# Cross-attention on one core: the order of the value passes, the engine of a subtraction, a second buffer, and where the bias is loaded

## The chip, the core and the metric

The kernel runs on one core of a Trainium2 chip. The metric is the device time of one execution in microseconds; the figure given for a kernel is the median of its runs. A profiled execution gives the trace from which the durations below are taken. Engines are named as in the profile: PE (TensorE matmuls), PEld (its weight loads), DVE (VectorE), ACT (ScalarE), POOL (GpSimd), SP (SyncE, which only issues transfers here).

## The reference

There are 32 batches of 512 queries with 640 channels, and 77 context tokens of 1024 channels for each batch. The inputs are float32.

```python
q = heads(x @ to_q_w)                    # 20 heads of 32 channels
k = heads(ctx[:, :77] @ to_k_w)
v = heads(ctx[:, :77] @ to_v_w)
h = softmax(q @ k.T / sqrt(32)) @ v      # the object, other and ip parts have no tokens here
out = merge(h) @ to_out_w + to_out_b + x
```

The context has exactly 77 tokens, so the three other attentions of the reference run over no keys and add nothing.

## The kernel before

**Numbers.** Matmul operands are held as two parts in a reduced float32 format: a high part (a rounding copy) and a low part (the source less the high part). A product is three matmuls: high by high, high by low, low by high (`PAIRS`). The helper `split` (L104 to L106) makes the parts: ACT copies the high part (L105), DVE subtracts for the low part (L106). Some places make the low part on POOL instead.

**The order is the program's own.** Every engine works its instructions in the order in which the code records them; nothing is rearranged. An instruction that waits holds up all that stands behind it on its engine. SP issues nearly all transfers, also in order.

**First stage: the context.** The 2464 context rows (32 x 77) go through in five groups `g` of 512 (the last has 416). `load_context` brings a group into `cs`, `context` transposes it (L169) and splits it into eight chunks `ct`, `keys` multiplies it with the key weights (L193, `pk`), `values_of` with the value weights (L193, `pv`), each for five chunks `j` of 128 channels, that is of four heads. `split_keys` splits a chunk of keys into `ks` and stores it to `k_dram` (L214). `split_values` transposes a chunk of values from PSUM into `vt` (L228), splits `vt` into slots 0 and 2 of `vs` (L231; slot 1 stays zero), and stores `vs` to `v_dram` with four transfers (L234). There is one `vt` and one `vs`. In a group, `split_values` of the chunks 0 to 3 stands ahead of the splits of the next group's context chunks 1 to 7, on ACT and on DVE. While a group is split, the query weights (`split_wq`) or the output weights (`split_wo`, stored to `wo_dram`, L323) are split between. The bias, one row of 640 spread over 128 partitions, is loaded at L310 in this stage, between the last weights and the second group's context.

**Second stage: 160 slots.** Slot `n` is batch `b` and chunk `j` of four heads. In it PE makes the scores of the slot, four tiles of 128 queries (`scores`, L452), and the queries of the next one (`queries`, L433). DVE takes the maximum of each tile (L460), ACT the exponentials (`exps`, L470). The slot also works on earlier slots:

- slot n-1: DVE inverts the sums (`sums`, L480), POOL multiplies (`normalize`, L485), DVE transposes the result into `z` (L492), SP stores it to `pd`, and `load_p` brings it back as `raw` with keys on the partitions (L508, L509);
- slot n-3 (`taken`): `cast_p` rounds the probabilities of the rows 0 to 255 of `raw` on ACT (L516: parts 0 and 1 of `pp`); `rest_p` rounds the 64 remaining rows on ACT (L522) and subtracts for parts 2 and 3 on DVE (L523); `last_p` subtracts for the 64 rows on POOL (L530). Part 4 of `pp` so holds the rest rows, high and low. `values` multiplies with the values `vb` (L544): for each half `p` of PSUM tile `pa` three passes, with the parts `p`, `2 + p` and 4. `sum_a` brings `pa` together into `aw` (ACT L555, DVE L557 twice), and `split_a` splits `aw` into `at`: ACT copies (L566), POOL subtracts (L567);
- the batch before: `piece` multiplies `at` with the output weights (L584, `po`), `finish` adds the residual and stores (L613), `add_bias` adds the bias to the residual on POOL (L577).

In some of the five slots of a batch the next batch's `x` is transposed on DVE (`transpose_x`, L256) and split, high on ACT and low on POOL (`split_x`, L263, L264). The order on the engines at the seam of two slots is: `sum_a`, exps of the last tile, `split_a`; then the next slot's `cast_p`, its first scores with L460, `rest_p`, `sums`, `normalize` and `last_p` (in the first slots, `last_p` ahead of `normalize`). The five value chunks of the last context group are made just before and in the first two slots (`context_values`). `end` finishes the last three takes.

Of the kernel before, what the change touches and what calls it, by code (L numbers as in the profile page):

```python
# [8 lines left out]
F32 = mybir.dt.float32  # L9
FPR = mybir.dt.float32r  # L10
AF = mybir.ActivationFunctionType
ALU = mybir.AluOpType
# [11 lines left out]
P = 128  # L24
Q = 32
HEADS = 20
HD = 32
# [24 lines left out]
def kernel(  # L52
# [25 lines left out]
    nc = tc.nc  # L78
    B, S, C = x.shape
# [6 lines left out]
    G = 512  # L86
# [5 lines left out]
    const = ctx.enter_context(tc.tile_pool(name="const", bufs=1))  # L92
# [5 lines left out]

    v_dram = dram.tile([NT + KPAD - NKEY, HPC, NC_, 3, HD], FPR, name="v_dram")
    wo_dram = dram.tile([P, NC_, 2, C], FPR, name="wo_dram")  # L100

    bias = const.tile([P, C], F32, name="bias")

    def split(hi, lo, src):  # L104
        nc.scalar.copy(hi, src)  # L105
        nc.vector.tensor_tensor(lo, src, hi.bitcast(F32), ALU.subtract)  # L106

    def load_weights(w, k0, kn, permuted=True, queues=(nc.sync,) * 4, tag="wraw"):


        raw = kvw.tile([P, 2, C], F32, tag=tag, name="wraw", bufs=3 if tag == "wraw" else 2)
        if permuted:
            rows = w.rearrange("(q c i) n -> q i c n", q=4, i=Q)
            for q, queue in enumerate(queues):
                queue.dma_start(raw[q * Q : (q + 1) * Q, :kn], rows[q, :, k0 : k0 + kn])
        else:
            rows = w.rearrange("(c p) n -> p c n", p=P)
            nc.sync.dma_start(raw[:, :kn], rows[:, k0 : k0 + kn])
        for k in range(kn):
            wraws[id(w), k0 + k] = raw[:, k]  # L120
# [15 lines left out]
    kvp = tc.alloc_tile_pool(name="kvp", bufs=1, side="right")  # L136
# [12 lines left out]
    cts, pks, pvs, css, craws, wraws = ({} for _ in range(6))  # L149
# [73 lines left out]
    def split_values(g, j, between=None):  # L223

        g0, gn = GROUPS_KV[g]
        na = gn // Q
        vt = kvp.tile([P, G], F32, tag="vt", name="vt", bufs=1)
        nc.vector.transpose(vt[:, :gn], pvs.pop(j)[:, :gn])  # L228
        if between is not None:
            between()  # L230
        split(vs[:, :na, 0], vs[:, :na, 2], vt[:, :gn].rearrange("p (a d) -> p a d", d=HD))  # L231
        dst = v_dram[g0 : g0 + gn, :, j].rearrange("(a t) i c d -> i t a (c d)", t=Q)
        for i in range(HPC):
            nc.sync.dma_start(  # L234
                dst[i].bitcast(F32),
                vs[i * Q : (i + 1) * Q, :na].rearrange("p a c d -> p a (c d)").bitcast(F32),
            )

    def context_values(g, j, pool):
        values_of(g, j, pool)  # L240
        split_values(g, j)
# [25 lines left out]
    ctx.enter_context(tc.manual_schedule(engines=ENGINES))  # L267


    vs = kvp.tile([P, G // Q, 3, HD], FPR, name="vs")  # L270
    nc.gpsimd.memset(vs.bitcast(F32), 0.0)
    zero = kvt.tile([P, 2, G], FPR, name="zero", tag="ks")[:, 0]
    nc.vector.memset(zero.bitcast(F32), 0.0)
    warm = psk.tile([P, G], F32, tag="ps", name="warm")
# [30 lines left out]
    for k in range(2, NK, 2):  # L305
        first(k, k + 1)
        if k < 6:
            load_weights(wk, k + 2, 2)
            load_weights(wv, k + 2, 2)
    nc.sync.dma_start(bias, bo.unsqueeze(0).to_broadcast([P, C]))  # L310
    LAST, split_ks = len(GROUPS_KV) - 1, []

    def split_wq():
# [16 lines left out]
    for g in range(LAST):  # L330
        for j in range(NC_):
            if g or j > 2:
                values_of(g, j, psk)
            if not g and j < 3:
                split_keys(0, j)
            if not g and j == 2:
                continue
            if j == 1:
                context(g + 1, 0)
            if not g and j == 3:  # L340
                split_values(0, 2)
                split_keys(0, 3)
            if j == NC_ - 1:
                if not g:
                    context(g + 1, 1, 2)
                    split_keys(0, 4)
                context(g + 1, *range(1 if g else 3, NK))
                if g + 1 == LAST:
                    kvw.release()
                    kvc.release()  # L350
                    xpool.append(
                        ctx.enter_context(
                            tc.tile_pool(name="xpool", bufs=1, reuse_waits="tile")
                        )
                    )
                    load_x(0)
            split_values(g, j, (None, split_wq, split_wo, None)[g])
# [28 lines left out]
    main = ctx.enter_context(tc.tile_pool(name="main", bufs=1, reuse_waits="tile"))  # L386
# [3 lines left out]

    raws, pps, ats, pds, sms, pqs, pas, aws, xrs, pos = ({} for _ in range(10))

    kbs, vbs, pnb = [], [], []
    for g, (j0, nj) in enumerate(GROUPS):
        kb = main.tile([P, nj, 2, KCOLS], FPR, name=f"kb{g}")
# [137 lines left out]

    PASSES = [(p, t, c) for p in range(2) for t, c in ((0, p), (0, 2 + p), (1, 4))]

    def values(n):
        b, j = divmod(n, NC_)
        g = GROUP_OF[j]  # L540
        pp, vb = pps.pop(n), vbs[g][:, j - GROUPS[g][0]]
        pas[n] = late[1].tile([P, 2, S], F32, tag="pa", name="pa", bufs=1)
        for m, (p, t, c) in enumerate(PASSES):
            nc.tensor.matmul(  # L544
                pas[n][:, p, :],
                vb[:, p, t, :],
                pp[:, c, :],
                start=(m % 3 == 0),
                stop=(m % 3 == 2),
            )  # L550

    def sum_a(n):
# [7 lines left out]
    def split_a(n):  # L560
        if n >= N - NC_ + 1:
            at = xpool[0].tile([P, 2, S], FPR, tag="xt", name="at", bufs=7)
        else:
            at = late[0].tile([P, 2, S], FPR, tag="at", name="at", bufs=8)
        aw = aws.pop(n)
        nc.scalar.copy(at[:, 0, :], aw[:, 0])  # L566
        nc.gpsimd.tensor_tensor(at[:, 1, :], aw[:, 0], at[:, 0, :].bitcast(F32), ALU.subtract)  # L567
        ats[n] = at

    def load_residual(b, t, xr=None):  # L570
# [66 lines left out]
    def take(m):  # L637
        values(m)
        sum_a(m)
        split_a(m)  # L640
# [14 lines left out]
    def slot(n, beside=()):  # L655
# [76 lines left out]
        if taken is not None:  # L732
            values(taken)
# [14 lines left out]
        if taken is not None:  # L748
            split_a(taken)
# [145 lines left out]
```

## Time and profile before

| | |
|---|---|
| median of 3 runs | 2183.4 us (2183.16 to 2183.89) |
| the profiled execution | 2184.32 us, its span in the profile 2182.5 us |
| PE | 1959.6 us busy (90%), mean granted clock 0.982 |
| ACT | 1545.2 us (71%) |
| DVE | 1414.8 us (65%) |
| POOL | 1207.1 us (55%) |
| first stage, up to the first slot's scores | about 314 us |
| L567, POOL's subtraction | 160 of 1293 ns, 206.9 us |
| L544, value matmuls | 960 |

A line of the waits reads: engine, tile and line of the one that waited, `<-` the one that ended the wait; total us, times, longest. A line of the timeline reads: start and duration in us, engine, line, operation, output from inputs with their shapes, and in brackets the idle time before it and who ended it. Matmuls overlap, so PE's busy time is not time at its peak; the pitch from start to start says more.

### The profile page before, as it was taken

The page shows a single profiled execution, that of the slowest core. Times are in us where ns is not written, and L with a number is a line of the kernel's source. Part 1 is how long each engine was busy: PE and PEld are TensorE (multiplying, and loading weights), DVE is VectorE, ACT ScalarE, POOL GpSimd, SP SyncE. Part 2 cuts the span into 40 slices and gives each one's busy share as a digit, 9 for nine tenths or more (in the row PEclk, how much of TensorE's full clock was granted, in tenths as well). Part 3 has the DMA queues.
Part 4 walks back from the last instruction along what each step waited for, and adds up shares of the span by engine and source line. Part 5 has one row for each costly group of instructions (what it writes and reads, how often), then busy time and mean ns, then how long its engine had stood idle before and what let it go on. Part 6 is the DMA issues. An engine that isn't in the chain of part 4 may idle for free. (4 is left out here: it accounts for less than half of the span.)

```text
span 2182.5 us, 36539 instructions
## 1 busy us (share of the span) xinstructions
PE 1959.6 (90%) x10332; PEld 1697.8 (78%) x10332; DVE 1414.8 (65%) x2174; ACT 1545.2 (71%) x6210; POOL 1207.1 (55%) x807
## 2 busy tenths in 40 slices
PE   9787987899999999999999999999999999999997
PEld 7566886777777777887778777787777877778786
DVE  4342344777777777777777777777777777777763
ACT  3131136887887877878788888888788887888872
POOL 1000024666666666666666666666666666666654
PEclk9899999999999999999999999999999999999998
DMA  9658677887878888888888788888888887877874
GB/s 190 147 149 212 153 158 206 218 204 205 204 202 206 203 208 206 209 204 204 208 205 208 197 211 209 205 201 206 208 207 207 205 201 204 203 203 206 202 187 133
DMA packets 568280, 431.28 MB, mean 198 GB/s; under 512 B 195344, under 2 KB 477072, under 8 KB 568080
## 3 DMA queue, kind: packets, MB, share of 16 engines
q1 hardware_dynamic: 564848, 417.65, 76.8%
q0 software_dynamic: 3136, 11.14, 1.4%
q8 instruction: 84, 1.38, 0.3%
q14 instruction: 116, 0.95, 0.1%
q10 hardware_dynamic: 96, 0.16, 0.0%
HBM read 247.17 MB, written 181.64 MB: 196 GB/s over the span
## 5 line engine op out<-in xcount | busy, mean ns | idle before, releaser
L470 ACT ACTIVATE pn<-sc,nm 128x77 f32<-128x77 f32 x2560 | 801.6, 333 | 74.1 <-DVE nm L460 70.2
L584 PE MATMUL po<-wo_s,at 128*128 128x320 f32 x3840 | 627.4, 312 | 10.2 <-DVE xr L613 3.6
L433 PE MATMUL pq<-xt,wq_s 128*128 128x512 f32 x2400 | 607.7, 394 | 0.6 <-POOL xt L264 0.6
L584 PEld LDWEIGHTS po<-wo_s,at 128*128 128x128 f32 x3840 | 579.4, 190 | 20.2 <-DVE xr L613 15.0
L470 ACT ACTIVATION_READ_ACCUMULATOR pn<-sc,nm 128x1 f32 x2560 | 541.3, 211 | 0.0
L433 PEld LDWEIGHTS pq<-xt,wq_s 128*128 128x128 f32 x2400 | 437.5, 189 | 76.9 <-POOL xt L264 1.7
L485 POOL TENSOR_TENSOR pn<-pn,rs 128x1232 f32<-128x1232 f32 x160 | 364.0, 2275 | 231.7 <-DVE rs L480 231.3
L567 POOL TENSOR_TENSOR at<-aw,at 128x512 fp32r<-128x512 f32 x160 | 206.9, 1293 | 417.4 <-ACT at L566 255.2
L460 DVE TENSOR_REDUCE nm<-sc 128x4 f32<-128x308 f32 x640 | 291.9, 457 | 215.1 <-PE sc L452 204.9
L544 PE MATMUL pa<-pp,vb 128*128 128x512 f32 x960 | 293.6, 415 | 149.7 <-POOL pp L530 146.2
L452 PE MATMUL sc<-kb,qt 128*128 128x308 f32 x1920 | 379.4, 306 | 14.9 <-ACT pn L470 13.3
L452 PEld LDWEIGHTS sc<-kb,qt 128*128 128x128 f32 x1920 | 325.1, 189 | 61.1 <-ACT pn L470 14.7
L523 DVE TENSOR_TENSOR pp<-raw,pp 128x1024 fp32r<-128x1024 f32 x160 | 252.5, 1578 | 173.8 <-ACT pp L516 173.8
L544 PEld LDWEIGHTS pa<-pp,vb 128*128 128x128 f32 x960 | 162.6, 189 | 233.6 <-POOL pp L530 215.1
L555 ACT COPY aw<-pa 64x1024 f32<-64x1024 f32 x160 | 161.9, 1012 | 223.0 <-PE pa L544 214.3
L492 DVE STREAM_TRANSPOSE z<-pn 128x1280 f32<-128x1280 f32 x160 | 241.8, 1511 | 120.1 <-POOL pn L485 89.2
L557 DVE TENSOR_TENSOR aw<-pa,aw 64x512 f32<-64x512 f32 x320 | 216.0, 675 | 30.0 <-ACT aw L555 27.7
L264 POOL TENSOR_TENSOR xt<-xs,xt 128x512 fp32r<-128x512 f32 x160 | 204.0, 1292 | 49.3 <-ACT xt L263 47.6
L530 POOL TENSOR_TENSOR pp<-raw,pp 64x512 fp32r<-64x512 f32 x160 | 208.1, 1301 | 20.6 <-ACT pp L522 8.6
L577 POOL TENSOR_TENSOR xr<-xr,bias 128x640 f32<-128x640 f32 x128 | 200.7, 1569 | 9.7
L193 PE MATMUL pk<-ct,wk_s 128*128 128x512 f32 (+1 forms) x600 | 146.2, 403 | 42.1 <-ACT ct L105 34.3
L193 PEld LDWEIGHTS pk<-ct,wk_s 128*128 128x128 f32 x600 | 119.2, 200 | 67.4 <-ACT ct L105 36.2
(42 smaller groups left out, 1415.7 us busy)
## 6 DMA issues: line engine op xcount, KB each, us to landing
pd<-z SPq DMA_DIRECT2D x640, 160.0 KB, 3.1
raw<-pd SPq DMA_DIRECT2D x160, 512.0 KB, 3.9
xs<-in_x_dram SPq DMA_DIRECT2D x128, 320.0 KB, 5.6
xr<-in_x_dram SPq DMA_DIRECT2D x128, 320.0 KB, 3.3
out_dram<-xr SPq DMA_DIRECT2D x127, 320.0 KB, 3.3
raw<-pd SPq DMA_DIRECT2D x160, 128.0 KB, 4.2
v_dram<-vs SPq DMA_DIRECT2D x80, 192.0 KB, 3.9
k_dram<-ks POOLq DMA_DIRECT2D x20, 512.0 KB, 3.4
```

What stands on the lines that cost most here:

```text
L193: nc.tensor.matmul(held[j][:, :gn], w[:, k, a, :], cts[g, k][:, c, :gn], start=(k == 0 and n == 0), stop=(k == NK - 1 and n == 2),)
L433: nc.tensor.matmul(pqs[n], wq_s[:, k, a, j * P : (j + 1) * P], xts[b, k][:, c, :], start=(k == 0 and m == 0), stop=(k == NC_ - 1 and m == 2),)
L452: nc.tensor.matmul(sc[:, :KCOLS], qt[:, a, t * P : (t + 1) * P], kb[:, j - GROUPS[g][0], c], start=(m == 0), stop=(m == 2),)
L460: nc.vector.tensor_reduce(nm, sc[:, :KCOLS].rearrange("p (h k) -> p h k", k=NKEY), AX.X, ALU.max, negate=True)
L470: nc.scalar.activation(pnb[n % 2][:, at, :NKEY], sc[:, i * NKEY : (i + 1) * NKEY], AF.Exp, bias=nm[:, i : i + 1], accum_out=sms[n][:, at : ...
L485: nc.gpsimd.tensor_tensor(pf, pf, rs.unsqueeze(2).to_broadcast([P, NQ * HPC, NKEY]), ALU.mult)
L492: nc.vector.transpose(z.rearrange("p b t j -> p t b j"), pn.rearrange("p (t h) k -> p t (h k)", t=NQ).rearrange("p t (b i) -> p t b i", i=Q),)
L523: nc.vector.tensor_tensor(pp[:, 2:4, :], raw[:, 0:2, :], pp[:, 0:2, :].bitcast(F32), ALU.subtract)
L530: nc.gpsimd.tensor_tensor(pp[64:, 4, :], raw[:64, 2, :], pp[:64, 4, :].bitcast(F32), ALU.subtract)
L544: nc.tensor.matmul(pas[n][:, p, :], vb[:, p, t, :], pp[:, c, :], start=(m % 3 == 0), stop=(m % 3 == 2),)
L557: nc.vector.tensor_tensor(aw[64 * p : 64 * p + 64, 0], pa[:64, p], aw[:64, p], ALU.add)
L584: nc.tensor.matmul(pos[b, t, h][:, :HALF], ats[b * NC_ + j][:, a, t * P : (t + 1) * P], wos[0][:, j, c, h * HALF : (h + 1) * HALF], start= ...
```

## The change

- `PASSES`: the six value matmuls of a slot are reordered. The two that read part 4 of `pp` come last; both PSUM halves are open at the same time.
- `split_a` uses `split`: the low part of `at` is now subtracted on DVE in place of POOL.
- Two buffers `vs`, used in turn by the chunk's number; the transpose writes straight into slot 2 of `vs`, and the low part is subtracted in place; `vt` is gone. Both buffers are cleared on POOL at the start.
- `bias` moves from the constant pool to the second stage's pool, and its load from the first stage to just ahead of the first `load_keys`. The tiles of the second stage lie 2.5 KB further in each partition; in the built program, POOL's clearing of the first key buffer now waits for PE, where before only that of the second did.

```diff
-    bias = const.tile([P, C], F32, name="bias")
...
     def split_values(g, j, between=None):
         g0, gn = GROUPS_KV[g]
         na = gn // Q
-        vt = kvp.tile([P, G], F32, tag="vt", name="vt", bufs=1)
-        nc.vector.transpose(vt[:, :gn], pvs.pop(j)[:, :gn])
+        vs = vss[j % 2]
+        vt = vs[:, :na, 2].bitcast(F32)
+        nc.vector.transpose(vt, pvs.pop(j)[:, :gn].rearrange("p (a d) -> p a d", d=HD))
         if between is not None:
             between()
-        split(vs[:, :na, 0], vs[:, :na, 2], vt[:, :gn].rearrange("p (a d) -> p a d", d=HD))
+        split(vs[:, :na, 0], vs[:, :na, 2], vt)
...
-    vs = kvp.tile([P, G // Q, 3, HD], FPR, name="vs")
-    nc.gpsimd.memset(vs.bitcast(F32), 0.0)
+    vss = [kvp.tile([P, G // Q, 3, HD], FPR, name=f"vs{n}") for n in range(2)]
+    for vs in vss:
+        nc.gpsimd.memset(vs.bitcast(F32), 0.0)
...
-    nc.sync.dma_start(bias, bo.unsqueeze(0).to_broadcast([P, C]))
...
+    bias = main.tile([P, C], F32, name="bias")
+    nc.sync.dma_start(bias, bo.unsqueeze(0).to_broadcast([P, C]))
     kbs, vbs, pnb = [], [], []
...
-    PASSES = [(p, t, c) for p in range(2) for t, c in ((0, p), (0, 2 + p), (1, 4))]
+    PASSES = [(p, 0, p + c) for p in range(2) for c in (0, 2)] + [(p, 1, 4) for p in range(2)]
...
                 vb[:, p, t, :],
                 pp[:, c, :],
-                start=(m % 3 == 0),
-                stop=(m % 3 == 2),
+                start=(c == p),
+                stop=(t == 1),
...
         aw = aws.pop(n)
-        nc.scalar.copy(at[:, 0, :], aw[:, 0])
-        nc.gpsimd.tensor_tensor(at[:, 1, :], aw[:, 0], at[:, 0, :].bitcast(F32), ALU.subtract)
+        split(at[:, 0, :], at[:, 1, :], aw[:, 0])
         ats[n] = at
```

## The prediction

> **What bounds the kernel now.** I read the waits first, then the timeline of one steady slot, then the timeline of the part before the slots. Of the waits:
>
> ```profile
> POOL at L567 <- ACT at L566: 255.2, 100, 4.9
> POOL pn L485 <- DVE rs L480: 231.3, 155, 18.2
> PEld pa L544 <- POOL pp L530: 215.1, 155, 3.7
> ACT aw L555 <- PE pa L544: 214.3, 154, 7.2
> DVE pp L523 <- ACT pp L516: 173.8, 159, 3.0
> PE pa L544 <- POOL pp L530: 146.2, 150, 3.3
> ACT vs L105 <- DMA v_dram<-vs: 84.5, 14, 9.3
> ```
>
> Columns are total us, times, longest. Every engine waits in every slot for the next one: PE for POOL's L530, ACT for PE's L544, DVE for ACT's L516, POOL for DVE's L480. No engine is full; one closed loop through all four sets the period. The timeline of a slot shows it:
>
> ```profile
> 488.13 0.48 DVE L460 TENSOR_REDUCE nm<-sc 128x4 f32<-128x308 f32 x1
> 488.19 0.62 ACT L566 CAST at<-aw 128x512 fp32r<-128x512 f32 x1 [0.24 <-DVE aw L557]
> 488.71 1.04 ACT L516 CAST pp<-raw 128x1024 fp32r<-128x1024 f32 x1
> 488.88 1.29 POOL L567 TENSOR_TENSOR at<-aw,at 128x512 fp32r<-128x512 f32 x1 [3.03 <-ACT at L566]
> 489.79 1.47 DVE L523 TENSOR_TENSOR pp<-raw,pp 128x1024 fp32r<-128x1024 f32 x1 [1.18 <-ACT pp L516]
> 491.50 2.28 POOL L485 TENSOR_TENSOR pn<-pn,rs 128x1232 f32<-128x1232 f32 x1 [1.32 <-DVE rs L480]
> 493.85 1.28 POOL L530 TENSOR_TENSOR pp<-raw,pp 64x512 fp32r<-64x512 f32 x1
> 493.98 0.63 PE L544 MATMUL pa<-pp,vb 128*128 128x512 f32 x2
> 495.18 1.20 PE L544 MATMUL pa<-pp,vb 128*128 128x512 f32 x4 [0.57 <-POOL pp L530]
> ```
>
> The loop: L566, L516, L523, L480, L485, L530, four value matmuls, then L555, L557 and L566 again. The six value matmuls are cut 2 + 4: the third is the first that reads the rest rows, and it starts 0.05 us after L530 ends. L567 starts with L516 and is not in the loop, but it overlaps L523. That costs:
>
> ```profile
> 357.64 1.22 DVE L523 TENSOR_TENSOR pp<-raw,pp 128x1024 fp32r<-128x1024 f32 x1 [3.02 <-ACT pp L516]
> ...
> 477.96 1.29 POOL L567 TENSOR_TENSOR at<-aw,at 128x512 fp32r<-128x512 f32 x1
> ...
> 478.32 2.01 DVE L523 TENSOR_TENSOR pp<-raw,pp 128x1024 fp32r<-128x1024 f32 x1 [0.47 <-ACT pp L516]
> ```
>
> L523 takes 1.22 us with POOL idle at its start, 1.47 where L567 runs 0.38 us into it, 2.01 where it runs 0.93 into it. In both overlapped rows L523 ends 1.08 us after L567, so VectorE does nothing while GpSimd holds on.
>
> The steady slots repeat every five (56.95 us), from the L530 that ends at 403.72 to the one at 2132.57: 1728.85 us, 30.4 periods. PE's wait between the second and third value matmul, less their normal 0.235 us pitch, is 0.55, 0.73, 1.13, 1.49, 1.75 us in the five slots.
>
> Before the slots, PE stands still at each group of the context:
>
> ```profile
> 207.90 0.62 ACT L105 CAST vs<-vt 128x512 fp32r<-128x512 f32 x1 [6.85 <-DMA v_dram<-vs]
> 209.27 2.79 SPq L234 DMA_DIRECT2D v_dram<-vs  x4
> 215.99 0.62 ACT L105 CAST vs<-vt 128x512 fp32r<-128x512 f32 x1 [6.85 <-DMA v_dram<-vs]
> 218.71 0.79 PE L193 MATMUL pk<-ct,wk_s 128*128 128x512 f32 x1 [12.79 <-ACT ct L105]
> ```
>
> The one vs is refilled only when its store has landed, some 7 us a chunk (8.1 here, where a wo store shares the queue); the next context chunk's cast stands behind that on ACT, and PE behind the cast. PE's stalls of this kind: 5.78 + 8.26, 8.89, 12.79 and 4.37, in sum 40.1 us.
>
> **The value passes.** Four matmuls now stand before the wait, two after. Now the third to sixth start 0.05, 0.39, 0.63 and 0.86 us after L530 and the last ends at 1.255; two would end at 0.39 + 0.40 = 0.79. The loop gains 0.465 us. The two moved ahead take 0.47, which fits the smallest stall, 0.55. PE's work per slot is unchanged.
>
> **VectorE's low part.** POOL loses 160 x 1.29 us that nobody waits for. DVE gains 160 x 0.65 (the same subtraction from SBUF, ct at L106: 653 ns), in order behind L557 and ahead of the next slot's L460 (0.48) and L523. It must wait for L566. Queued behind it: that L460, whose maximum is wanted only after L516 and L522, and L523, which is in the loop. From L566's end (488.81): DVE starts at +0.03 (as L523 does after L516), ends at +0.68; L460, overlapping 0.08 as neighbours on DVE do, ends at +1.08; L523 can start at +1.01. Today L516 releases it at +0.98. So ScalarE's cast covers the insertion but for 0.03. Then L523 takes 1.22 instead of 1.47, as POOL is idle: it ends at +2.22 instead of +2.44. Gain 0.22. Bounds: -0.1 (L523 as long as now, and late) to +0.28. I take 0.22, from the 1.22 row. If L516's cover were gone, the whole 0.65 + 0.40 would be on the path.
>
> One slot in five is worse. There POOL's three xt subtractions (474.20, 3.79 us) run until 5.41 us after L530's end, but L566 would end at 4.76 - 0.465 = 4.295. The new subtraction waits 1.115 for POOL, ends 0.515 after that, and L460 and L523 follow: +3.17 instead of today's +2.98. That slot gains 0.465 - 0.19 = 0.27; bounds 0 to 0.5.
>
> Sum: 4 x (0.465 + 0.22) + 0.27 = 3.0 us a period, 30.4 periods: 91 us. Next late would be PE: the 0.73 stall falls to 0.04, the others stay open; ACT's shortest idle time before L555 is 0.59, with 0.3 more in front of its second exps, and DMA's share rises from 0.81 to 0.86. With the ends of the bounds: 1.2 (0.365 x 4, and -0.24) to 3.5 a period, 38 to 106 us.
>
> [...]
>
> **Two vs buffers.** A chunk now waits for the store before the last, and it is VectorE's transpose that waits, not ScalarE's copy. Queued behind it on DVE are the same splits as today. The transpose's strided output I leave at 0.70 (L169 and L492 also stride). Stores issued one after the other land about 1.0 us apart, 4.1 a chunk. Second group: first store issued 125.71, landed 132.3; second landed 136.4; the fourth chunk's copy at 137.2 instead of 146.65, 9.5 earlier, so all of 8.89 goes. First group: 67.8 with a k store between, copy at 68.6 instead of 80.76: 12.2 of the 14.04. Third, with wo stores: 205.8 instead of 215.99: 10 of 12.79. Fourth: 4.4, all. Sum 35.5 us. After each stall the matmuls run at a 427 ns pitch instead of 227 for a while: the 105 that follow take 26.4, 25.9 and 27.0 us, not 23.8, and the fourth group loses 2.0. I count this whole where the stall goes and half where 1.8 and 2.8 us stay: 2.1 + 2.0 + 1.3 + 1.6 = 7. Together 42 us; bounds 14 (stores queue so that a third of the stalls goes) and 50 (all).
>
> [...]
>
> In the first slots the last chunk's copy waits 9.31 us for its store (ACT, 347.05) and PE 5.58 behind it (350.09): 5.6 gained. The second memset, 1.4 us on POOL, delays eight wv loads, whose copies (ACT, 8.26 and 12.90) PE first reads at 13.92 and 19.36: taken as 0, at most 1.4.
>
> **Bias later.** Its load leaves a place where nothing waited and stands on SP between the last k store and the first kb loads, which land at 313.51 to 314.19; PE's scores start at 314.31. No cover: 327 KB at 190 GB/s, 1.7 us. First used at 403.8. So 5.6 - 1.7 = 4 net, bounds -2 to 8. The first kb memset now waits for PE, 1.1 us; kb's loads were issued 5 us later behind other SP work, so 0.
>
> **The end.** The last pieces wait 0.85 us for L567 once, and one value pass moves earlier: 1.5, bounds 0 to 2.5.
>
> **Sum.** 91 + 42 + 4 + 1.5 = 138.5. The profiled execution took 2184.3 us (span 2182.5 and 1.8 around it): 2045.8. The median of the runs is 0.9 less: 2045.
>
> **Rivals.** (1) The loop closes elsewhere for L523: GpSimd's absence does not shorten it, so only the order pays: 63 + 42 + 5.5, 2073. For: nothing but the few 1.22 to 1.45 rows of the first slots shows a free L523. 18%. (2) The stores bound the context stage and the wait only moves to DVE: 14 for 42, 2073. For: DMA share 0.56 to 0.72 there, far from idle. 13%. (3) More is freed, as the PE stalls left (2.6 a period) and the clock allow: about 2015. 6%. (4) Slower: the new subtraction and the L460 behind it lie wholly on the loop, 1.05 + 0.03 less 0.465, 0.615 x 152 = 93 lost against 47.5 gained elsewhere: 2229. It decides for slower once the path grows by 0.465 + 0.31 = 0.78 a slot. Against it: L516's 1.04 us, which runs at that time on another engine. 4%. (5) No change, these cancelling: 1%. The forecast has 58%.
>
> The range reaches over rivals 1 and 2 and the bounds of the terms, short of all bad ends at once (2117): 2018 to 2105. A measurement of this kernel can tell about 0.2%, 4.4 us, from no change. Faster 0.95, same 0.01, slower 0.04.
>
> **What would show it.** Right: 54 us for five slots; pa's matmuls cut 4 + 2, the wait under half its 146 us; L523 near 1.22; L567's successor on DVE just ahead of an L460; no PE stall over 3 us between the groups. Wrong: L523 still 1.47; L523 released by DVE's own queue more than 0.2 us after L516; PE stalls that now name DVE's transpose waiting for v_dram.

## The result, and the profile after

The kernel after takes 2056.65 us (median of 4 runs, 2056.36 to 2058.63), against 2183.49 us before: ratio 0.9421, 95% interval 0.9405 to 0.9437. The forecast was 2045, in a range from 2018 to 2105. The profiled execution's span is 2054.2 us instead of 2182.5: 128.3 us less, where the sum said 138.5.

Cut at the two marks that the prediction used (the L530 of the fifth and of the 157th take; the line is L531 after), the gain stands like this, in us:

| stretch of the span | before | after | gain | forecast |
|---|---|---|---|---|
| to the first scores | 314.32 | 272.37 | 41.95 | 42 |
| first slots, to the first mark | 89.40 | 83.71 | 5.7 | 4 |
| steady slots, between the marks | 1728.85 | 1649.42 | 79.4 | 91 |
| end | 49.93 | 48.7 | 1.2 | 1.5 |
| five steady slots | 56.91 | 54.30 | 2.61 | 3.0 |

So all that is missing lies in the steady slots. The waits of the kernel after (total us, times, longest; most lines left out):

```profile
POOL pn L486 <- DVE rs L481: 442.5, 94, 11.6
...
ACT aw L556 <- PE pa L545: 164.9, 156, 8.3
DVE at L104 <- ACT at L103: 135.3, 160, 1.0
...
PEld pa L545 <- POOL pp L531: 127.8, 153, 3.4
...
PE pa L545 <- POOL pp L531: 55.8, 82, 2.9
...
DVE vs L227 <- DMA v_dram<-vs: 19.2, 7, 4.5
```

PE's wait for the rest rows fell from 146.2 to 55.8 us, as foretold under half. The wait for the store of vs (84.5 us on ACT before) is 19.2 us and now DVE's. The first line is long because POOL has lost work and arrives early; by itself that costs nothing. The timeline of one steady slot (start, duration, engine, line; idle time before it and who ended it in brackets; here and in the later timelines, rows that play no part are left out, also where no dots stand):

```profile
990.88 0.62 ACT L103 CAST at<-aw 128x512 fp32r<-128x512 f32 x1 [0.98 <-DVE aw L558]
991.41 1.05 ACT L517 CAST pp<-raw 128x1024 fp32r<-128x1024 f32 x1
991.53 0.69 DVE L104 TENSOR_TENSOR at<-aw,at 128x512 fp32r<-128x512 f32 x1 [0.74 <-ACT at L103]
992.14 0.47 DVE L461 TENSOR_REDUCE nm<-sc 128x4 f32<-128x308 f32 x1
992.53 1.22 DVE L524 TENSOR_TENSOR pp<-raw,pp 128x1024 fp32r<-128x1024 f32 x1
993.66 0.25 DVE L481 RECIPROCAL rs<-sm 128x16 f32<-128x16 f32 x1
...
994.05 2.27 POOL L486 TENSOR_TENSOR pn<-pn,rs 128x1232 f32<-128x1232 f32 x1 [5.75 <-DVE rs L481]
...
996.26 1.09 PE L545 MATMUL pa<-pp,vb 128*128 128x512 f32 x4
...
996.41 1.28 POOL L531 TENSOR_TENSOR pp<-raw,pp 64x512 fp32r<-64x512 f32 x1
...
997.74 0.73 PE L545 MATMUL pa<-pp,vb 128*128 128x512 f32 x2 [0.39 <-POOL pp L531]
```

The value matmuls are cut 4 + 2 and end 0.785 us after L531 (before 1.255). DVE's new subtraction and L461 fit under ACT's L517 as worked out: L524 starts 1.03 us after the cast into at, takes 1.22 and ends 2.25 after it (forecast 2.22, before 2.45). But look at the reciprocal and normalize: L481 ends at 993.91 (its start and 0.25), L486 starts at 994.05, 0.144 us later. Before, L480 and L485 stood 0.078 us apart:

```profile
1003.46 0.24 DVE L480 RECIPROCAL rs<-sm 128x16 f32<-128x16 f32 x1
...
1003.78 2.27 POOL L485 TENSOR_TENSOR pn<-pn,rs 128x1232 f32<-128x1232 f32 x1 [1.33 <-DVE rs L480]
```

The prediction does not have this step, and it is in the loop in every slot. The built program shows a difference there too. Before, 153 of the 160 normalize instructions wait for DVE alone: L567, ahead of them on POOL, had already waited for an ACT instruction later than the exponentials. After, with no L567, 123 wait for DVE and ACT, 31 for DVE, ACT and an earlier POOL instruction. The starts follow: 0.144 us with two waits, about 0.17 in the slots with three. The trace shows where the time goes. An instruction of its own on POOL's sequencer, which only waits, now stands ahead of every normalize (kernel before, then after; duration in ns as smallest, median and largest, then first and last start in us):

```profile
L485 POOLq EVENT_SEMAPHORE  x7: 17/17/43, 328.3 to 2139.7; - x7
L486 POOLq EVENT_SEMAPHORE  x160: 17/17/43, 285.3 to 2011.9; - x160
```

In the kernel after, it is this instruction that waits for DVE, the wait that ends last, and normalize itself waits for ACT, which has long been done. It ends 0.052 us after the reciprocal, and normalize starts 0.092 us after that. Where it waits for both DVE and ACT it takes 0.043 instead of 0.017 us.

### The profile page after: what moved, and what is told of

It is laid out like the page before. It is cut to its first block, busy times and chain, and to the rows that moved or that the text cites. A ratio compares the mean times of both kernels' runs of the same rounds, so it can differ in the third digit from the quotient of the medians.

```text
span 2054.2 us, 36186 instructions
## 1 busy us (share of the span) xinstructions
PE 1952.5 (95%) x10332; PEld 1694.3 (82%) x10332; DVE 1464.6 (71%) x2334; ACT 1547.1 (75%) x6210; POOL 1002.7 (49%) x648
## 4 chain that ended last, share of the span: by engine, by line
PE 36%; DVE 15%; issue 15%; DMA 12%; POOL 10%; ACT 6%; SPq 5%; POOLq 0%; ACTq 0%; DVEq 0%
PE po L584 11%; PE pq L434 9%; PE pa L545 6%; POOL pn L486 6%; PE sc L453 5%; DMA pd<-z 5%; DVE pp L524 4%; POOL pp L531 4%; DMA raw<-pd 3%; DVE aw L558 3%; SPq L500 2%; DVE z L493 2%; PE pk L191 2%; DVE nm L461 2%; ACT at L103 2%
## 5 line engine op out<-in xcount | busy, mean ns | idle before, releaser
L486 POOL TENSOR_TENSOR pn<-pn,rs 128x1232 f32<-128x1232 f32 x160 | 364.0, 2275 | 736.0 <-DVE rs L481 442.5
L461 DVE TENSOR_REDUCE nm<-sc 128x4 f32<-128x308 f32 x640 | 291.2, 456 | 132.3 <-PE sc L453 132.2
L545 PE MATMUL pa<-pp,vb 128*128 128x512 f32 x960 | 291.0, 415 | 66.0 <-POOL pp L531 55.8
L104 DVE TENSOR_TENSOR at<-aw,at 128x512 fp32r<-128x512 f32 x160 | 138.7, 867 | 135.3 <-ACT at L103 135.3
L531 POOL TENSOR_TENSOR pp<-raw,pp 64x512 fp32r<-64x512 f32 x160 | 208.7, 1305 | 51.5 <-ACT pp L523 39.5
L524 DVE TENSOR_TENSOR pp<-raw,pp 128x1024 fp32r<-128x1024 f32 x160 | 194.3, 1215 | 6.5 <-ACT pp L517 6.5
L517 ACT CAST pp<-raw 128x1024 fp32r<-128x1024 f32 x160 | 168.7, 1055 | 3.7 <-DMA raw<-pd 3.7
L103 ACT CAST at<-aw 128x512 fp32r<-128x512 f32 x160 | 99.8, 624 | 71.8 <-DVE aw L558 71.5
```

Source lines behind the costliest of these rows:

```text
L461: nc.vector.tensor_reduce(nm, sc[:, :KCOLS].rearrange("p (h k) -> p h k", k=NKEY), AX.X, ALU.max, negate=True)
L486: nc.gpsimd.tensor_tensor(pf, pf, rs.unsqueeze(2).to_broadcast([P, NQ * HPC, NKEY]), ALU.mult)
L524: nc.vector.tensor_tensor(pp[:, 2:4, :], raw[:, 0:2, :], pp[:, 0:2, :].bitcast(F32), ALU.subtract)
L531: nc.gpsimd.tensor_tensor(pp[64:, 4, :], raw[:64, 2, :], pp[:64, 4, :].bitcast(F32), ALU.subtract)
L545: nc.tensor.matmul(pas[n][:, p, :], vb[:, p, t, :], pp[:, c, :], start=(c == p), stop=(t == 1),)
```

## Experiments

Each is an edit of the kernel before or after, except that L613 ahead of the transpose builds on the kernel with the rest rows first; times are medians of four runs (ten for the late bias alone), ratios are against the kernel before, run on the same chip. Gains of single slots are differences of the median length of that slot over some 30 repeats.

**The order alone** (kernel before):

```diff
-    PASSES = [(p, t, c) for p in range(2) for t, c in ((0, p), (0, 2 + p), (1, 4))]
+    PASSES = [(p, 0, p + c) for p in range(2) for c in (0, 2)] + [(p, 1, 4) for p in range(2)]
...
-                start=(m % 3 == 0),
-                stop=(m % 3 == 2),
+                start=(c == p),
+                stop=(t == 1),
```

> The kernel before with the new order of the value passes and nothing else. Theory (the loop through ACT, DVE, POOL and PE sets the period): the tail after L530 falls from 1.255 to 0.79 us, 0.465 us in each of 152 slots, 71 us: 2112 us, 54.6 us for five slots; POOL's normalize goes on starting 0.08 us after the reciprocal. Rival (PE is next late, and the missing 12 us of the whole change were lost to it): the order alone brings no more than 59 us, 2124 us, 55.0 us for five slots.

Measured: 2115.5 us (0.9690, 0.9675 to 0.9704), 54.74 us for five slots, normalize 0.078 us after the reciprocal in four slots of five; the steady stretch lost 66.1 us. Close to the theory, and the rival's 59 is excluded in the steady stretch. Four slots gained 0.45 to 0.46, as the 0.465 says; the slot j = 3 gained 0.38. This is the prediction's one slot in five in which POOL's three xt subtractions run late; it is called the contested slot below. Its timeline shows why:

```profile
1023.16 1.23 DVE L523 TENSOR_TENSOR pp<-raw,pp 128x1024 fp32r<-128x1024 f32 x1 [0.18 <-ACT pp L516]
1023.26 2.29 POOL L567 TENSOR_TENSOR at<-aw,at 128x512 fp32r<-128x512 f32 x1
1024.31 0.24 DVE L480 RECIPROCAL rs<-sm 128x16 f32<-128x16 f32 x1
...
1025.51 2.27 POOL L485 TENSOR_TENSOR pn<-pn,rs 128x1232 f32<-128x1232 f32 x1
```

Here L523 starts 0.10 us ahead of L567 and keeps its 1.23 us, and L567 pays: 2.29 instead of 1.29. Normalize stands behind L567 on POOL, 0.96 us after a reciprocal that is long done.

**The low part on DVE alone** (kernel before):

```diff
-        nc.scalar.copy(at[:, 0, :], aw[:, 0])
-        nc.gpsimd.tensor_tensor(at[:, 1, :], aw[:, 0], at[:, 0, :].bitcast(F32), ALU.subtract)
+        split(at[:, 0, :], at[:, 1, :], aw[:, 0])
```

> The kernel before with the low part of the attention on DVE and nothing else. Theory (without POOL's subtraction, normalize has to wait for ACT's exponentials itself, beside DVE's reciprocal, and starts later): four slots in five gain 0.22 and one loses 0.19, 21 us, and every slot loses 0.066 to 0.10, 10 to 15 us: 2172 to 2178 us, normalize 0.14 us after the reciprocal. Rival (the missing 12 us were lost to PE, after the order was changed): alone this edit brings its 21 us, 2162 us, normalize 0.08 us after the reciprocal.

Measured: 2159.6 us (0.9884, 0.9868 to 0.9900), 56.15 us for five slots. The time is the rival's, the mechanism the theory's. Normalize does start 0.144 us after the reciprocal, and the four ordinary slots gain only 0.13 to 0.18 each, not 0.22. But the contested slot gains 0.20 where the expectation had it lose 0.19: that loss had been taken from the whole change, in which the copy into at comes earlier and so deeper into POOL's three xt subtractions. Alone, DVE's subtraction takes 1.17 us there (1.63 in the kernel after), L523 takes 1.21 instead of 2.01 and ends 2.72 us after the cast into at, against 2.99 before. L523's group has hardly a wait left, and its mean is that of an unstretched row (kernel before, then this one; count, busy us and mean ns, then idle time before it):

```profile
L523 DVE TENSOR_TENSOR pp<-raw,pp 128x1024 fp32r<-128x1024 f32 x160 | 252.5, 1578 | 173.8 <-ACT pp L516 173.8
L523 DVE TENSOR_TENSOR pp<-raw,pp 128x1024 fp32r<-128x1024 f32 x160 | 194.3, 1214 | 3.6 <-ACT pp L516 3.6
```

**The first stage alone** (kernel after with the other two parts undone; start and stop go back with `PASSES`):

```diff
-    PASSES = [(p, 0, p + c) for p in range(2) for c in (0, 2)] + [(p, 1, 4) for p in range(2)]
+    PASSES = [(p, t, c) for p in range(2) for t, c in ((0, p), (0, 2 + p), (1, 4))]
...
-        split(at[:, 0, :], at[:, 1, :], aw[:, 0])
+        nc.scalar.copy(at[:, 0, :], aw[:, 0])
+        nc.gpsimd.tensor_tensor(at[:, 1, :], aw[:, 0], at[:, 0, :].bitcast(F32), ALU.subtract)
```

> The kernel before with two vs buffers, the transpose in place and the late bias, and nothing else. Theory: all of the 47.6 us by which the kernel after comes earlier to the steady slots is theirs: 2136 us, the period unchanged at 56.9 us. Rival (a part of it is due to the shorter loop in the first slots, of which there are eight, 0.5 us each): 2140 us.

Measured: 2139.3 us (0.9795, 0.9780 to 0.9809), period 56.93 us, the first mark 45.0 us earlier. Nearer the rival's number, but not for the rival's reason: with the order alone the first mark stays where it was (403.71 against 403.72), so the shorter loop brings nothing in the first slots. What differs is scatter of the first stage itself: in the profiles of nine kernels that share it, the first scores start between 272.12 and 275.49 us, and those of the kernel after are among the earliest.

**The low part on POOL again** (kernel after):

```diff
-        split(at[:, 0, :], at[:, 1, :], aw[:, 0])
+        nc.scalar.copy(at[:, 0, :], aw[:, 0])
+        nc.gpsimd.tensor_tensor(at[:, 1, :], aw[:, 0], at[:, 0, :].bitcast(F32), ALU.subtract)
```

> The kernel after with the low part of the attention made on POOL again. Theory (the DVE edit brings 21 us and costs 10 to 15 through normalize's later start): 2056.6 + 6 to 11 = 2063 to 2068 us, 54.6 us for five slots, normalize 0.08 us after the reciprocal, L523 at 1.47 us again. Rival (DVE's edit brings its 21 us whole, and the missing 12 us are in the order): 2078 us.

Measured: 2072.5 us (0.9488, 0.9474 to 0.9502), 54.72 us for five slots; in the four ordinary slots L524 is at 1.47 again and normalize at 0.08 again. Between the two expectations. In the steady stretch DVE's edit is worth 12.7 us on top of the order, against 23.1 alone. Slot by slot it gives 0.14 to 0.18 in four and takes 0.17 in the contested one, so nearly all of the difference between the two figures is the contested slot: +0.20 alone, -0.17 together.

**A tiny POOL instruction that waits for ACT** (kernel after):

```diff
+    nap = const.tile([P, 8], F32, name="nap")
...
         split(at[:, 0, :], at[:, 1, :], aw[:, 0])
+        nc.gpsimd.tensor_tensor(nap, at[:, 0, :8].bitcast(F32), at[:, 0, :8].bitcast(F32), ALU.subtract)
```

> The kernel after, with one tiny subtraction on POOL (8 columns) that reads ACT's copy at behind split_a. Normalize then needs to wait for DVE alone again, as in the kernel before. Theory (normalize starts later in the kernel after because it has a second wait, for ACT): it starts 0.08 us after the reciprocal instead of 0.144 to 0.18, 0.066 us in four slots of five and 0.10 in one, 0.36 in a period, 11 us: about 2046 us, 53.95 us for five slots. Rival (it starts later because POOL has been idle for long before it): POOL still idles 2.9 us between the tiny subtraction and the reciprocal, the start stays at 0.14 us, 2057 us.

**The same, waiting for DVE:**

```diff
-        nc.gpsimd.tensor_tensor(nap, at[:, 0, :8].bitcast(F32), at[:, 0, :8].bitcast(F32), ALU.subtract)
+        nc.gpsimd.tensor_tensor(nap, at[:, 1, :8].bitcast(F32), at[:, 1, :8].bitcast(F32), ALU.subtract)
```

> The same tiny subtraction on POOL, but reading the low part that DVE makes; normalize keeps its second wait, for ACT. Theory (second wait): normalize still starts 0.144 us after the reciprocal, 2057 us, 54.3 us for five slots. Rival (long idle time): POOL now idles only some 2.3 us, the start falls to 0.08 us, 2046 us.

Measured: 2046.4 us (0.9367, 0.9353 to 0.9381) with the instruction that waits for ACT, 2057.8 us (0.9415, 0.9399 to 0.9431) with the one that waits for DVE; 53.96 and 54.31 us for five slots. The timelines of both, first the one that waits for ACT:

```profile
990.58 0.71 POOL L569 TENSOR_TENSOR nap<-at 128x8 f32<-128x8 f32 x1 [3.27 <-ACT at L103]
...
992.67 0.25 DVE L482 RECIPROCAL rs<-sm 128x16 f32<-128x16 f32 x1
992.99 2.28 POOL L487 TENSOR_TENSOR pn<-pn,rs 128x1232 f32<-128x1232 f32 x1 [1.70 <-DVE rs L482]
```

```profile
996.89 0.20 POOL L569 TENSOR_TENSOR nap<-at 128x8 f32<-128x8 f32 x1 [4.00 <-DVE at L104]
...
998.25 0.24 DVE L482 RECIPROCAL rs<-sm 128x16 f32<-128x16 f32 x1
998.64 2.28 POOL L487 TENSOR_TENSOR pn<-pn,rs 128x1232 f32<-128x1232 f32 x1 [1.55 <-DVE rs L482]
```

POOL idles 1.70 us before normalize in the first and 1.55 in the second, so its idle time is nearly the same; only the wait for ACT differs. In the first kernel normalize starts 0.078 to 0.080 us after the reciprocal in 153 slots, in the second 0.143 to 0.145 in 153. The separate waiting instruction ahead of normalize is there 7 times in the first kernel, as in the kernel before, and 160 times in the second. The wait is the cause, the idle time is not. Removing it gives 10.3 us of the steady stretch back (1649.42 to 1639.17), and this kernel is faster than both kernels of the change.

**The contested slot made like the others** (kernel after):

```diff
-            xr = late[0].tile([P, C], F32, tag="xr", name="xr", bufs=3)
+            xr = late[0].tile([P, C], F32, tag="xr", name="xr", bufs=4)
...
-    RESIDUAL = {1: (1, 0), 2: (1, 1), 3: (1, 2), 4: (1, 3)}
-    BIAS = {2: (1, 0), 3: (1, 1), 4: (1, 2), 0: (2, 3)}
+    RESIDUAL = {0: (1, 0), 1: (1, 1), 3: (1, 2), 4: (1, 3)}
+    BIAS = {1: (1, 0), 2: (1, 1), 4: (1, 2), 0: (2, 3)}
```

> The kernel after, with the bias additions of POOL moved from the slots j = 2 and 3 to j = 1 and 2 (their residual rows are loaded one slot earlier, in four buffers). In the slot j = 3 POOL's three xt subtractions then start 1.57 us earlier and end before ACT's copy at. Theory (the loop sets the period in that slot too): L524 ends 2.25 us after at instead of 3.19, 0.95 us a period, 29 us: 2028 us. Rival (PE is next late there: it waits only 0.08 us ahead of the fifth value matmul): between 0.08 and 0.19 us a period, 2 to 6 us: 2051 to 2054 us.

Measured: 2054.3 us (0.9398, 0.9384 to 0.9412), 54.10 us for five slots, 0.20 less. PE is next late, as the rival says. The slot j = 3 itself gains the whole 0.95 (11.42 to 10.48), and the next one loses 0.77 (10.32 to 11.09). In the next slot L531 no longer sets PE's start:

```profile
488.41 1.92 PE L584 MATMUL po<-wo_s,at 128*128 128x320 f32 x12
488.88 1.29 POOL L531 TENSOR_TENSOR pp<-raw,pp 64x512 fp32r<-64x512 f32 x1
490.17 1.56 PE L545 MATMUL pa<-pp,vb 128*128 128x512 f32 x6
```

All six value matmuls run in one piece behind PE's own output matmuls.

**Both edits together** (the two diffs above of `nap` with ACT and of `RESIDUAL` and `BIAS`, with three residual buffers):

> The edits of both: the tiny subtraction that reads ACT's copy, and the bias additions of j = 2 and 3 one slot earlier (three residual buffers). Loop everywhere: 2017 us. PE next late in the slot j = 3: 0.27 us a period from four slots and 0.08 to 0.19 from that one, 2043 to 2046 us.

Measured: 2049.5 us (2044.3 to 2050.2; 0.9373, 0.9359 to 0.9387), 53.90 us for five slots. That is above the 2043 to 2046 expected, and not to be told from 2046.4: against that kernel the steady stretch is 2.0 us shorter and the first mark 3.9 us later.

**The rest rows ahead of normalize** (kernel after; it would take the 2.3 us of normalize out of PE's wait):

```diff
-        if taken is not None and not has_out:
+        if taken is not None:
             last_p(taken)
         if n:
             normalize(n - 1, rs)
-        if taken is not None and has_out:
-            last_p(taken)
```

> The kernel after, with POOL's subtraction of the rest rows (L531) ahead of normalize in every slot, as it already stands in the first slots. The value matmuls then need not wait for the reciprocal and normalize, and normalize's wait for ACT is covered by L531's. Theory (the loop through normalize is all that PE waits for): L531 ends near L524's end, 4 us earlier; PE's waits ahead of the fifth value matmul, 0.08 + 0.16 + 0.55 + 0.87 + 1.15 = 2.8 us in five slots, go: 51.5 us for five slots, 85 us less, about 1972 us. Rival (another path through the same engines is next late: L531 runs beside DVE's L524, normalize and the transpose into z start up to 1 us later, and DVE's split of qt stands behind them): the period stays at 54.3 us or grows by up to 0.5 us a slot: 2057 to 2133 us.

Measured: 2170.1 us (0.9926, 0.9906 to 0.9946), 57.96 us for five slots, worse than even the rival's bound. PE's wait before the value matmuls is gone, but normalize starts later behind L531, the transpose into z waits for it, and L613, which frees the output banks, stands behind that on DVE. Once in five slots PE stands still:

```profile
1004.70 2.27 POOL L486 TENSOR_TENSOR pn<-pn,rs 128x1232 f32<-128x1232 f32 x1
...
1007.00 1.51 DVE L493 STREAM_TRANSPOSE z<-pn 128x1280 f32<-128x1280 f32 x1 [2.65 <-POOL pn L486]
...
1008.44 0.65 DVE L104 TENSOR_TENSOR qt<-pq,qt 128x512 fp32r<-128x512 f32 x1
1009.01 0.87 DVE L613 TENSOR_TENSOR xr<-po,xr 128x320 f32<-128x320 f32 x2
...
1009.54 5.17 PE L584 MATMUL po<-wo_s,at 128*128 128x320 f32 x18 [3.21 <-DVE xr L613]
```

The 18 output matmuls then take 5.17 us; their granted clock is the 0.50 in this line of stretches (from:to, length, busy time of PE, PEld, DVE, ACT and POOL with the number of instructions, granted clock, DMA share, GB/s):

```profile
1009.00:1014.50 5.50, 4.96 (x18) 4.96 (x19) 3.24 (x7) 4.05 (x13) 3.82 (x4) 0.50 0.78 227
```

**L613 ahead of the transpose** (that kernel, with PE's order unchanged):

```diff
+        if has_out and j == 3:
+            piece(bo_, first)
+            finish()
         if n and has_out:
             transpose_p(n - 1)
...
         if has_out:
-            piece(bo_, first)
+            if j != 3:
+                piece(bo_, first)
...
-        if j == 3:
-            finish()
```

> The kernel with the rest rows ahead of normalize (2170 us), and in the slot j = 3 the two residual additions L613 on DVE moved ahead of the transpose into z; PE's order is the same. There PE stood still 3.2 us once in five slots, until L613 freed the output bank, and then ran the next 20 output matmuls at a pitch of 0.27 instead of 0.146 us, 2.4 us more. Theory (moving a step before normalize is right, and L613 behind the late transpose was all that went wrong): 57.96 - 5.6 = 52.3 us for five slots, 30.4 periods: 2170 - 172 = 1998 us, below every kernel so far. Rival (the transpose into z, 1.7 us later in every slot, is itself on a path of PE: through the split of qt behind it or through its way back as raw): 55 us or more for five slots, 2080 us or more.

Measured: 2072.1 us (0.9486, 0.9470 to 0.9502), 54.83 us for five slots. The 3.2 us stall is gone and 98 us with it, but the rival holds for the rest: PE now stands 2.25 us for an L613 of another slot and mostly 0.3 to 0.7 us for the split of qt, both behind the late transpose. Ahead of L531, normalize feeds two paths back to PE; putting it later shortened one and lengthened the other by more.

**The bias late, alone** (kernel before):

```diff
-    bias = const.tile([P, C], F32, name="bias")
...
-    nc.sync.dma_start(bias, bo.unsqueeze(0).to_broadcast([P, C]))
...
+    bias = main.tile([P, C], F32, name="bias")
+    nc.sync.dma_start(bias, bo.unsqueeze(0).to_broadcast([P, C]))
     kbs, vbs, pnb = [], [], []
```

> The kernel before with the bias loaded late and nothing else. The prediction's term: the load stands ahead of the first kb loads, PE's first scores wait 1.7 us longer: 2185 us. Rival (the scores wait for the queries and their split, not for kb): 0, 2183.5 us. The time can't tell these apart; the profile can, by when kb lands, when PE ends the queries and when the first scores start.

Measured: 2185.5 us (1.0004, 0.9995 to 1.0013). In the profile kb has landed at 314.70 and the first scores start at 315.52; the queries' last matmul ends 8.88 us before that, against 8.89 in the kernel before. Between them PE multiplies a chunk of context values, without a pause. The first scores come 1.2 us later than in the kernel before (315.52 against 314.32), but that is not the load's doing: the queries already start 1.2 us later (303.05 against 301.83), and the bias is issued only at 305.83. The rival is right, the load costs nothing here.

## Why the prediction was right, and where its sum was off

**The value passes: right.** The tail of 0.785 us and the gain of 0.45 to 0.46 a slot are the steps as put; alone 66 us where 0.465 x 152 gives 71, the rest lost in the contested slot to L567 ahead of normalize.

**VectorE's low part: mechanism right, size off.** That ACT's L517 covers the insertion, that L523 falls to 1.22 and ends 0.2 us earlier, and that L523 ends near +3.17 in the contested slot (measured 3.19) all came out. The step that failed is the one sentence "POOL loses 160 x 1.29 us that nobody waits for". L567's duration was free in the ordinary slots; its wait was not. It had waited for ACT in normalize's place. Without it normalize carries that wait and starts 0.066 us later, about 0.09 with three waits: 0.34 in a period, 10.3 us by the pair of tiny instructions above. The term of 0.22 an ordinary slot so measured 0.14 to 0.18. The loss of 0.19 in the contested slot measured 0.17, partly by luck: with the order alone L523 already ended early there, and it was normalize that came 0.95 us late. With the wait given back, the steady stretch gains 89.7 us where the sum said 91.

**Two vs buffers: right in sum, partly by luck.** The stalls of the second and the fourth group are gone. The two that should stay at 1.8 and 2.8 us are 3.13 and 2.41. So two of the prediction's own signs went against this term: a stall of over 3 us is left between the groups, and both stalls go back to DVE's transpose waiting for v_dram (2.53 and 3.60 us). The one of 2.41 reads so:

```profile
180.74 0.72 DVE L227 STREAM_TRANSPOSE vs<-pv 128x512 f32<-128x512 f32 x1 [3.60 <-DMA v_dram<-vs]
181.53 0.62 ACT L103 CAST vs<-vs 128x512 fp32r<-128x512 f32 x1 [4.26 <-DVE vs L227]
183.59 1.21 ACT L103 CAST ct<-craw 128x512 fp32r<-128x512 f32 x2 [1.44 <-DVE craw L167]
184.26 0.49 PE L191 MATMUL pk<-ct,wk_s 128*128 128x512 f32 x1 [2.41 <-ACT ct L103]
184.98 5.30 PE L191 MATMUL pk<-ct,wk_s 128*128 128x512 f32 x15 [0.23 <-DVE ct L104]
```

It is the chain foretold: the store, now DVE's transpose, ACT's copies, PE. The gain of 41.95 matches 42, but the same stage in the other kernels gives 38.8 to 42.2.

**First slots.** The copy no longer waits for its store, but PE still stands 4.89 us there (before 5.58), because the next transfer in SP's order is late instead: ACT's L517 waits 3.67 us for raw, whose load was issued behind eight stores of values. The term "5.6 gained" was mostly not gained at that place, and "bias costs 1.7" was not lost. The second error was a misread: kb landed 0.12 us before the scores began and was taken for their releaser, while PE had been busy up to that moment. The first stage alone gives 4.2 of the 5.7 us in this stretch; which of its smaller steps they come from is not shown.

**The rivals.** Rival 1 (GpSimd's absence does not shorten L523) is refuted by L523's group: a mean of 1.21 us where it was 1.58. No run shows the 63 us that this rival gave the steady slots; the order alone, with L523 at a mean of 1.43 us, gained 66.1 us there. Rival 3 (more is freed) met its limit in PE: the contested slot's 0.95 us, once freed, came back as 0.77 in the next slot. Rivals 2 and 4 did not occur: the first stage gained what was said, and L517 covered DVE's new work but for 0.05 us (L524 starts 1.03 us after the cast into at, before 0.98). One figure of the prediction's range does not follow from its bounds: all bad ends at once add up to a gain of 38 + 14 - 2 + 0 = 50, which is 2133 us and not 2117.

**The overlap of DVE and POOL, and the clock.** In the rows here in which a subtraction on DVE and one on POOL overlapped, the later one paid: in the kernel before L523 took 2.01 instead of 1.22 us behind L567, L567 took 2.29 instead of 1.29 us behind L523 (in the row of the order alone), L531 1.79 instead of 1.28 us beside L524 in the kernel with the rest rows first. Moving the subtraction from POOL to DVE was worth 24 us alone: L523 is no longer stretched (a mean of 1.21 instead of 1.58 us), and DVE's new 0.69 us lies under ACT's cast.

The clock: after the stall of 2.41 us the matmuls ran at a pitch of 427 instead of 227 ns for eight matmuls, 3.4 us, and so did eight after the stall of 3.13 us; the granted clock was 0.50 from 185.20 to 188.61 us and from 72.56 to 75.97 us. After the 3.21 us stall of the kernel with the rest rows first, 18 matmuls took 5.17 us at a granted clock of 0.50. The mean clock of that kernel is 0.945 over 2170.0 us, that of the kernel after 0.991 over 2054.2; by an estimate from these figures the first spent some 200 us more at half clock, near 7 us for each of about 30 such stalls. In the kernel with L613 ahead of the transpose the mean is 0.987 over 2070.4 us, about 54 us at half clock by the same estimate, or 16 times 3.4 us; PE waited there 32 times for L613, 70.6 us in sum and 2.5 at the longest, so at most about half of these stalls can have been followed by 3.4 us at half clock. For the short stalls the prediction counted half (1.3 and 1.6 us); measured were eight matmuls at 0.2 us more, 1.6 us for each stall.

## What to carry to other kernels

An instruction that is taken off an engine takes its waits with it, and the next instruction there inherits those that nothing else covers. So ask of a removed step not only who waits for its result, but for whom it had waited in the name of those behind it; a tiny instruction with the right input, off the path, can carry that wait again (here 10.3 us of the steady stretch). And when a loop through four engines is shortened, look at the smallest of the waits it leaves, here 0.08 us, before counting on more: past it the next bound takes the gain back one slot later (here 0.77 of 0.95 us).

## What was not expected of the hardware

With a second semaphore wait, a POOL instruction started 0.066 us later (0.144 us after the reciprocal instead of 0.078), even where the added wait had long been met, and the same after 1.55 us and after 5.75 us of idle time; with a third wait about 0.03 more. The time lies in the separate waiting instruction: here it was given the wait that ends last. Whether less is lost when it gets the early one is not shown.

PE's stalls between 2.2 and 3.2 us differ in what follows them, and the record of the granted clock shows a reason that the length of the stall hides. In the traces of the kernels before and after, the clock changes only at multiples of one step of 3.41 us. Of the steps at full clock in these two traces, the 20 in which PE stood for 1.73 us or more in sum were each followed by a step at half clock; none with at most 1.66 us was. In the kernel after, the stall of 2.41 us lay inside one step, which had 2.64 us of standing in all, and the half clock followed. The one of 3.13 us fell across two: the step with its first 1.63 us was followed by full clock, the next, with 1.73 us in all, by half clock. In the kernel with the rest rows first, the matmuls behind a stall of 3.2 us ran at a pitch of 0.27 instead of 0.146 us, 2.4 us more for 20 of them. So in these traces where a short stall falls counts as well as how long it is.
